# Cross-attention on one core: score weights by eleven block products in 64x64 tiles, and a loop of long and short steps

## The chip, the core and the metric

The kernel runs on one core of a Trainium2 chip, all in float32. The metric is device time in microseconds, lower is better. The engines are TensorE (PE in the profile, its weight loads PEld), VectorE (DVE), ScalarE (ACT), GpSimd (POOL) and SyncE (SP), which starts most of the transfers.

## The reference

There are B = 16 batches of 256 queries `x` (width 256) and 77 context rows `c` (width 192), and H = 8 heads of width 256. The mask is all ones. Cut to what matters:

```python
Q = (x @ Wq).reshape(B, -1, H, 256).transpose(0, 2, 1, 3)
K = (c @ Wk).reshape(B, -1, H, 256).transpose(0, 2, 1, 3)
V = (c @ Wv).reshape(B, -1, H, 256).transpose(0, 2, 1, 3)
score = jnp.einsum('bhqd,bhkd->bhqk', Q, K) / sqrt(256)
attn = softmax(where(mask, score, -inf), axis=-1)
out = einsum('bhqk,bhkd->bqhd', attn, V).reshape(B, -1, H * 256) @ Wo + x
return (out - mean(out)) * rsqrt(var(out) + 1e-5) * gamma + beta
```

## The kernel before

*Weights are combined first.* Per head, G = Wq Wk^T / 16 and U = Wv Wo are made once. G lies in `gA` (its first 128 context columns) and `gB` (the other 64, two heads to a tile), c turned in `cA` and `cB` in the same way. Then only A = G c ("a" tiles), scores = x A, and out = attn (c U) remain. A is made by groups of GB = 4 batches (NG = 4 groups): a *place* is two heads of one group, 16 places in all. `prepare_a` makes a place with 128x32 tiles over `cA` (L193) and 64x32 tiles over `cB` (L205), 308 columns each, into PSUM tiles `pa`, and ACT copies them out (L963). c U of one batch (`vw`) is `prepare_vw` (L227, L238).

*A step* is one batch b + 1: two tiles t of 128 queries. `scores` (L303, two PSUM banks per tile), `shift` (DVE, L320: adds the mask and keeps each head's greatest score, and releases the bank), `exponential` (ACT, L340), reciprocal (L355) and `weigh` (POOL, L361), `turn` (DVE transpose, L371). Then, for the batch before, `seven` (PE, L450): attn times `vw` for both tiles by seven block products instead of eight, into two banks `pm` and `po`; it needs `sums` of the turned weights (POOL, L431 to L434, tile `ss`) and `differences` of `vw` (POOL, L414, tile `ts`). ACT copies `pm` out as `m` (L475); `add_seven` adds `po` to x on DVE (`add_product`, L498) and `m` on POOL (L484). After that come mean and variance (`finish`, L506 and L509), `spread` (ACT, L527 and L528), and `normalise` (DVE, L548 and L577).

*Order.* PE, DVE, ACT, POOL and SP each run their instructions strictly as the program writes them (a manual schedule). The loop runs over b from -1 to 14; every second step ("ahead") prepares `vw` of two batches and two places of A. PE's order in a pair of steps is scores, `pv`, `pa`, `pv`, `pa`, `pv`, `pa`, `pv`, `pa`, `seven`, scores, `seven`. The 8 PSUM banks have one tag, `mm`, and go round: a product that takes a bank waits for whoever read the bank's last content. `turn_last` (L293) turns the last rows of `vw`, `transpose_x` (L165) the x tiles of a group ahead; `load_x` and `load_xT` start their transfers on SP.

## Time and profile before

| | |
|---|---|
| median of 3 runs | 271.01 us (270.75 to 271.03) |
| profiled execution, its span | 269.95 us, 268.2 us |
| busy, PE | 262.5 us |
| busy, PEld (weight loads) | 191.8 us |
| busy, DVE | 185.9 us |
| busy, POOL | 173.2 us |
| busy, ACT | 157.6 us |

The page gives the busy time of each engine; a row of a view of groups gives line, engine, operation, output and inputs, tile shape, count, then busy us and mean ns of one. A row of a timeline gives start, length, engine, line and count, and in brackets the idle time ahead with what ended it. Lengths of merged PE rows contain the end of a pipelined matmul, so the distance of two starts is the better measure. L numbers are lines of the kernel before.

### The profile page before, as it was taken

How to read it: one execution, taken by the hardware profiler on the slowest of the kernel's cores; microseconds unless marked ns; L12 is line 12 of the kernel's file. 1: busy time of each engine (PE TensorE's matmuls, PEld its weight loads, DVE VectorE, ACT ScalarE, POOL GpSimd, SP SyncE). 2: the span in 40 equal slices, each digit the busy share in tenths (PEclk: the TensorE clock that was granted, in tenths of full speed). 3: DMA queues.
4: the chain of work that ended last, by engine and by line, in shares of the span. 5: the costliest groups of instructions: out<-in, count | busy, mean ns of one | idle time of the engine just before them, and what ended most of it. 6: DMA issues, size and time to landing. Idle time of an engine off the chain costs nothing.

```text
span 268.2 us, 14455 instructions
## 1 busy us (share of the span) xinstructions
PE 262.5 (98%) x6090; PEld 191.8 (72%) x6090; DVE 185.9 (69%) x808; ACT 157.6 (59%) x667; POOL 173.2 (65%) x240
## 2 busy tenths in 40 slices
PE   8999999999999999999999999999999999999992
PEld 8566578944984699459944995499669957985662
DVE  1555967493583868665886379647977887799785
ACT  3243336536857565955596468737775595636772
POOL 1042005728399739994799669965998799585452
PEclk9999999999999999999999999999999999999999
DMA  6989987901500130232012401340034010100112
GB/s 190 217 199 228 334 138 142 311 21 34 129 7 2 46 80 2 63 111 71 5 43 90 112 5 43 91 113 2 6 120 122 4 45 2 44 22 22 46 40 80
DMA packets 41696, 22.69 MB, mean 85 GB/s; under 512 B 24144, under 2 KB 40608, under 8 KB 41632
## 3 DMA queue, kind: packets, MB, share of 16 engines
q1 hardware_dynamic: 41248, 20.98, 30.1%
q0 software_dynamic: 384, 0.79, 1.3%
q8 instruction: 48, 0.79, 1.3%
q14 instruction: 16, 0.13, 0.2%
HBM read 17.57 MB, written 4.19 MB: 81 GB/s over the span
## 4 chain that ended last, share of the span: by engine, by line
PE 98%; DVE 1%; issue 0%; DVEq 0%
PE ps L303 25%; PE pa L193 13%; PE pv L227 11%; PE po L450 11%; PE pm L450 8%; PE pa L205 6%; PE pv L238 6%; PE po L383 4%; PE pu L773 3%; PE pr L263 2%; PE pgb L834 2%; PE pw L787 1%; PE idle L703 1%; PE pr L274 1%; PE phb L850 1%; PE po L399 1%
## 5 line engine op out<-in xcount | busy, mean ns | idle before, releaser
L340 ACT ACTIVATE s<-s,top 128x77 f32<-128x77 f32 x256 | 85.3, 346 | 44.2 <-DVE top L320 37.9
L303 PE MATMUL ps<-a,xT 128*32 128x154 f32 x2048 | 69.9, 294 | 0.0
L303 PEld LDWEIGHTS ps<-a,xT 128*32 128x32 f32 x2048 | 66.2, 110 | 1.2 <-issue 0.4
L361 POOL TENSOR_TENSOR p<-s,rden 128x512 f32<-128x512 f32 x64 | 47.5, 768 | 29.5 <-DVE rden L355 29.4
L320 DVE CUSTOM_DVE_ANT_0 s<-ps,bias 128x77 f32<-128x77 f32 x256 | 43.5, 232 | 14.3 <-PE ps L303 14.3
L340 ACT ACTIVATION_READ_ACCUMULATOR s<-s,top 128x1 f32 x224 | 42.0, 187 | 0.0
L193 PE MATMUL pa<-cA,gA 128*32 128x308 f32 (+1 forms) x576 | 36.6, 395 | 0.0
L193 PEld LDWEIGHTS pa<-cA,gA 128*32 128x32 f32 x576 | 18.3, 110 | 21.0 <-issue 7.0
L484 POOL TENSOR_TENSOR xg<-xg,m 128x256 f32<-128x256 f32 x39 | 28.7, 736 | 6.6 <-DVE xg L498 4.5
L577 DVE SCALAR_TENSOR_TENSOR xg<-xg,rstd,bet 128x256 f32<-128x256 f32 x27 | 22.9, 847 | 14.0 <-ACT rstd L528 12.6
L227 PE MATMUL pv<-uA,cA 128*32 128x512 f32 x256 | 30.6, 595 | 0.0
L371 DVE STREAM_TRANSPOSE pT<-p 128x640 f32<-128x640 f32 x32 | 25.5, 821 | 3.4 <-POOL p L361 3.3
L414 POOL TENSOR_TENSOR ts<-vw 128x768 f32<-128x768 f32 x13 | 24.0, 1848 | 5.9 <-ACT vw L963 5.9
L963 ACT COPY vw<-pv 128x512 f32<-128x512 f32 x32 | 17.8, 584 | 14.8 <-PE pv L227 8.3
L498 DVE TENSOR_TENSOR xg<-po,xg 128x256 f32<-128x256 f32 x31 | 11.5, 405 | 13.8 <-PE po L450 13.3
L320 DVE DVE_READ_ACCUMULATOR2_ANT top<- 128x1 f32 x256 | 20.8, 81 | 0.0
L205 PE MATMUL pa<-cB,gB 64*32 64x308 f32 (+2 forms) x512 | 20.4, 387 | 0.0
L963 ACT COPY a<-pa 128x308 f32<-128x308 f32 (+1 forms) x56 | 18.9, 395 | 1.9 <-PE pa L193 0.4
L205 PEld LDWEIGHTS pa<-cB,gB 64*32 64x32 f32 (+1 forms) x512 | 11.0, 110 | 11.4 <-issue 6.2
L548 DVE SCALAR_TENSOR_TENSOR xg<-xg,mv,gam 128x256 f32<-128x256 f32 x30 | 17.6, 588 | 0.1
L238 PE MATMUL pv<-uB,cB 64*32 64x512 f32 x256 | 17.3, 597 | 0.0
L227 PEld LDWEIGHTS pv<-uA,cA 128*32 128x32 f32 x256 | 7.5, 109 | 12.8 <-issue 9.9
(119 smaller groups left out, 404.1 us busy)
## 6 DMA issues: line engine op xcount, KB each, us to landing
xg<-in_x_dram SPq DMA_DIRECT2D x8, 512.0 KB, 4.4
xT<-in_x_dram SPq DMA_DIRECT2D x56, 64.0 KB, 2.6
out_dram<-xg SPq DMA_DIRECT2D x11, 256.0 KB, 2.2
wo<-in_L_xattn_Wo_dram SPq DMA_DIRECT2D x4, 512.0 KB, 7.8
wq_blk<-in_L_xattn_Wq_dram SPq DMA_DIRECT2D x12, 128.0 KB, 4.3
out_dram<-xg SPq DMA_DIRECT2D x10, 128.0 KB, 1.9
wk_blk<-in_L_xattn_Wk_dram SPq DMA_DIRECT2D x12, 96.0 KB, 3.6
wvT<-in_L_xattn_Wv_dram POOLq DMA_DIRECT2D x8, 96.0 KB, 6.6
```

The source lines that it names most:

```text
L193: nc.tensor.matmul(flat(o[i * BK : (i + 1) * BK]), gA[:, h, cols(dc, i)], flat(cA[:, batches, :]), start=not rest_first and n in opening, ...
L205: nc.tensor.matmul(flat(banks[j + k][i * BK : (i + wide) * BK]), gB[half(k), h // 2, dc * P + i * BK : dc * P + (i + wide) * BK], flat(cB[ ...
L227: nc.tensor.matmul(pv[k][i * BK : (i + 1) * BK], cA[:, b, k * BK : (k + 1) * BK], uA[:, parts, :, i], start=not rest_first, stop=rest_first,)
L238: nc.tensor.matmul(pv[k][i * BK : (i + 1) * BK], cB[half(k), b, k * BK : (k + 1) * BK], uB[half(k), parts, :, i], start=rest_first, stop=n ...
L303: nc.tensor.matmul(ps[m // 2][i * BK : (i + 1) * BK, m % 2 * 2 * S2 : (m % 2 + 1) * 2 * S2], xT_of[t // PT][:, j * NM + m, dc], flat(a_of[ ...
L320: nc.vector.tensor_tensor_reduce(s[:, h], ps[a][:, k * S2 : (k + 1) * S2], bias[:, b, :], scale=-1.0, scalar=FAR, op0=ALU.add, op1=ALU.min ...
L340: nc.scalar.activation(s[:, h], s[:, h], AF.Exp, bias=top[:, one], scale=-1.0, accum_out=den[:, one] if summed_by_act(t) else None,)
L361: nc.gpsimd.tensor_tensor(part, e_mh[:, :, :, keys], rden_mh.unsqueeze(3).to_broadcast(list(part.shape)), ALU.mult,)
L371: nc.vector.transpose(pT_of[t].rearrange("p n m q -> p m n q"), p.rearrange("p m (n k) -> p m n k", k=BK),)
L450: nc.tensor.matmul(out[i * BK : (i + 1) * BK], weight[:, i], moving, start=first and n == 0, stop=final and n == len(terms) - 1,)
L484: nc.gpsimd.tensor_tensor(to, to, what, ALU.add)
L963: nc.scalar.copy(dst, src)
```

## The change

`prepare_fast` makes A for groups 1 to 3 (ten places with the whole of two heads; what is left of the last group goes the old way). Per head, G and c are seen as blocks of 64, A as 2x2 blocks (over dc, and over two halves of the four batches) plus the remaining 64 context columns; with sums of blocks of G (`gS`, `gC`) and of c (`cT`, `cD`) made ahead on ACT and POOL, 11 block products take the place of 12. Each is 64x64 and 154 columns wide; two heads are interleaved so that tiles at opposite corners of the array alternate. Per head there are two PSUM banks, `mids` and `ends` (tiles `pf`). The first product of each `mids` bank is copied out by ACT and its place used again; `put_together` makes the blocks of A by four additions on DVE.

The loop of the first 10 steps is written anew as `long_step` and `short_step`. In the long step PE's order is scores, `pv` over cA for two batches, `seven`, `pv` over cB, two fast places; the short step has scores and `seven`. In `scores_and_masks`, the mask pass of the first tile goes ahead of the preceding short step's last turn, sums and `add_seven` (`between`). Mean and variance of tiles of batches below 7 are made on ScalarE from accumulated sums. `normalise` is moved into later places, and the sums of c for the next group into two long steps.

**POOL, where a long step begins (b + 1 = 4; `ss_3` and `m_2`, `xg_1` are of the step before, `p` the weights of tiles 8 and 9).** Before:

```order
L361 TENSOR_TENSOR p_1_86<-s_7_1620,rden_7_1659 128x4x26
L414 TENSOR_TENSOR ts_3_1667<-vw_3_1378 128x768
L484 TENSOR_TENSOR m_2_1735<-m_2_1735 128x128 x2
L484 TENSOR_TENSOR xg_1_518<-xg_1_518,m_2_1735 128x256
L484 TENSOR_TENSOR xg_1_518<-xg_1_518,m_2_1735 128x2x128
L484 TENSOR_TENSOR xg_1_518<-xg_1_518,m_2_1735 128x256
L431 TENSOR_TENSOR ss_3_1750<-pT_7_1741 128x256
L432 TENSOR_TENSOR ss_3_1750<-pT_7_1741,pT_6_1739 128x256
L433 TENSOR_TENSOR ss_3_1750<-pT_7_1741,ss_3_1750 128x256
L434 TENSOR_TENSOR ss_3_1750<-pT_6_1739,ss_3_1750 128x256
L361 TENSOR_TENSOR p_0_85<-s_8_1823,rden_8_1917 128x4x128
L361 TENSOR_TENSOR p_0_85<-s_8_1823,rden_8_1917 128x4x26
```

With the change:

```order
L602 TENSOR_TENSOR ss_3_1916<-pT_7_1914 128x256
L603 TENSOR_TENSOR ss_3_1916<-pT_7_1914,pT_6_1831 128x256
L604 TENSOR_TENSOR ss_3_1916<-pT_7_1914,ss_3_1916 128x256
L605 TENSOR_TENSOR ss_3_1916<-pT_6_1831,ss_3_1916 128x256
L655 TENSOR_TENSOR m_2_1814<-m_2_1814 128x128 x2
L655 TENSOR_TENSOR xg_1_532<-xg_1_532,m_2_1814 128x256
L655 TENSOR_TENSOR xg_1_532<-xg_1_532,m_2_1814 128x2x128
L655 TENSOR_TENSOR xg_1_532<-xg_1_532,m_2_1814 128x256
L532 TENSOR_TENSOR p_0_88<-s_8_1904,rden_8_2188 128x4x128
L532 TENSOR_TENSOR p_0_88<-s_8_1904,rden_8_2188 128x4x26
L532 TENSOR_TENSOR p_1_89<-s_9_1928,rden_9_2192 128x4x128
L532 TENSOR_TENSOR p_1_89<-s_9_1928,rden_9_2192 128x4x26
```

The weighing of tile 7 (`p_1`, `s_7`) and `ts_3` now come ahead of this stretch; the sums `ss_3` go ahead of `m_2` and `xg_1`, and the weighing of both tiles of the long step stands behind all of them.

**DVE, behind the reciprocals of the same step (`po_3` is the bank that `seven` filled, `xT_3` an x tile of a group ahead).** Before:

```order
L355 RECIPROCAL rden_9_1933<-den_9_1921 128x8
L548 SCALAR_TENSOR_TENSOR xg_1_518<-xg_1_518,mv_0_1346,gam_69 128x256
L577 SCALAR_TENSOR_TENSOR xg_1_518<-xg_1_518,rstd_4_1944,bet_90 128x256
L371 STREAM_TRANSPOSE pT_8_2086<-p_0_85 128x4x5x32
L371 STREAM_TRANSPOSE pT_9_2088<-p_1_86 128x4x5x32
L165 STREAM_TRANSPOSE xT_3_1441<-xT_3_1441 128x512 x2
L548 SCALAR_TENSOR_TENSOR xg_1_518<-xg_1_518,mv_0_1346,gam_69 128x256
L577 SCALAR_TENSOR_TENSOR xg_1_518<-xg_1_518,rstd_4_1944,bet_90 128x256
L498 TENSOR_TENSOR xg_1_518<-po_3_2017,xg_1_518 128x256 x2
```

With the change:

```order
L526 RECIPROCAL rden_8_2188<-den_8_1938 128x8
L526 RECIPROCAL rden_9_2192<-den_9_1947 128x8
L542 STREAM_TRANSPOSE pT_8_2196<-p_0_88 128x4x5x32
L542 STREAM_TRANSPOSE pT_9_2198<-p_1_89 128x4x5x32
L669 TENSOR_TENSOR xg_1_532<-po_3_1990,xg_1_532 128x256 x2
L725 SCALAR_TENSOR_TENSOR xg_0_530<-xg_0_530,mv_0_1569,gam_69 128x256
L754 SCALAR_TENSOR_TENSOR xg_0_530<-xg_0_530,rstd_2_1964,bet_93 128x256
L174 STREAM_TRANSPOSE xT_3_1620<-xT_3_1620 128x512 x2
L372 TENSOR_TENSOR a_2_2073<-pf_2_0_0_2074,a_2_2073 128x2x77
L372 TENSOR_TENSOR a_2_2073<-pf_2_0_0_2074,a_2_2073 128x4x77
L372 TENSOR_TENSOR a_2_2073<-pf_2_0_0_2074,a_2_2073 128x2x77
L372 TENSOR_TENSOR a_2_2073<-pf_2_0_0_2075,a_2_2073 128x6x77
```

The statistics are gone, the two additions of `po_3` (L669) stand directly behind the turns of tiles 8 and 9, and behind the moved normalise and x turns come the new additions of `put_together` (L372), the first four of twelve.

**PE, the end of `seven` and the first fast place (`pf_2_0_0`, `pf_2_1_1`: banks of heads 0 and 1 of group 2; waits in brackets name the engine that PE waits for).** Before, the rows with waits of `pv` and `pa` ahead of `seven`, and the first row behind them:

```order
L303 MATMUL ps_9_1_1790<-a_1_838,xT_2_960 32x154 [waits DVE_49,PE_49]
L227 MATMUL pv_4_0_1850<-uA_79,cA_81 32x512 [waits DVE_49,PE_49]
L227 MATMUL pv_4_1_1851<-uA_79,cA_81 32x512 [waits DVE_49,PE_49]
L193 MATMUL pa_2_0_0_0_1853<-cA_81,gA_77 32x308 [waits Activation_49]
L193 MATMUL pa_2_1_0_0_1854<-cA_81,gA_77 32x308 [waits DVE_49,PE_49]
L193 MATMUL pa_2_0_1_0_1855<-cA_81,gA_77 32x308 [waits DVE_49,PE_49]
L193 MATMUL pa_2_1_1_0_1856<-cA_81,gA_77 32x308 [waits DVE_49,PE_49]
L238 MATMUL pv_4_0_1850<-uB_80,cB_82 32x512
```

With the change, the end of `seven`, the last row of `pv`, and of the fast place the rows with waits and some that follow them:

```order
L621 MATMUL po_3_1990<-vw_3_1362,ss_3_1916 32x128 [waits Pool_49]
L621 MATMUL po_3_1990<-vr_804,pT_7_1914 32x256 x4
L621 MATMUL po_3_1990<-ts_3_1606,pT_7_1914 32x128 x8
L403 MATMUL pv_5_0_1971<-uB_83,cB_85 32x512
L360 MATMUL pf_2_0_0_2075<-cA_84,gA_77 64x154 [waits DVE_49,PE_49]
L360 MATMUL pf_2_0_0_2074<-cA_84,gA_77 64x154 [waits DVE_49,PE_49]
L360 MATMUL pf_2_1_1_2077<-cA_84,gA_77 64x154 [waits Activation_49]
L360 MATMUL pf_2_1_1_2076<-cA_84,gA_77 64x154 [waits DVE_49,PE_49]
L360 MATMUL pf_2_1_1_2077<-cA_84,gS_519 64x154
L360 MATMUL pf_2_0_0_2075<-cT_79,gA_77 64x154
L360 MATMUL pf_2_1_1_2077<-cT_79,gA_77 64x154
```

Where the products of A waited for ACT and for banks that DVE's mask passes release, the third pair of the fast place's products (`pf_2_1_1_2076`) now takes the bank of `po_3` and waits for the second addition of L669.

```diff
--- before.py
+++ after.py
+    KX = HB * S2
+    FAST = NG - 1
+    low, high = slice(0, LB), slice(LB, P)
+    cT = const.tile([P, 4, FAST, KX], F32, tag="cT", name="cT")
+    cD = const.tile([P, FAST, KX], F32, tag="cD", name="cD")
+    gC = const.tile([P, NF, P], F32, tag="gC", name="gC")
...
-            return slice((2 * i + dc) * BK, (2 * i + dc + 1) * BK)
+            return slice(dc * P + i * BK, dc * P + (i + 1) * BK)
...
+    def sums_of_g():
+        for parts, sums, e, own, other in parts_of_g():
+            nc.scalar.copy(sums[own, 0, e], parts[other, 1, e])
+            nc.scalar.copy(gC[own], gB[other, :, P:])
+        for parts, sums, e, own, other in parts_of_g():
+            s1, s2, s3 = (sums[own, n, e] for n in range(3))
+            add(s1, s1, parts[own, 1, e])
+            subtract(s2, s1, parts[own, 0, e])
+            subtract(s3, parts[own, 0, e], parts[own, 1, e])
...
+    def sums_of_c(lo, hi):
+        xs, ys = halves_of(cA, lo, hi)
+        t1, t2, t3, t4 = (cT[:, n, lo - 1 : hi - 1] for n in range(4))
+        subtract(t1, ys, xs)
+        for own, other in ((low, high), (high, low)):
+            nc.gpsimd.tensor_copy(t2[own], ys[other])
+        subtract(t3, t2, ys)
+        subtract(t2, t2, t1)
+        for own, other in ((low, high), (high, low)):
+            nc.gpsimd.tensor_copy(t4[own], t2[other])
+        subtract(t4, xs, t4)
...
+        for e, h in enumerate(heads):
+            for banks in (mids, ends):
+                banks.append(ps_mm.tile([P, 3, KX], F32, tag="mm", name=f"pf_{g}_{h}_{len(ends)}"))
...
+        def middle(e):
+            h, own = heads[e], (high, low)[e]
+            return [
+                ((mids[e], 2), from_g(own, h, 0), c_of(cA, own, xs)),
+                ((mids[e], 0), from_s(own, 0, h), t_of(own, 0)),
+                ((mids[e], 2), from_s(own, 1, h), t_of(own, 1)),
+                ((mids[e], 1), from_s(own, 2, h), t_of(own, 2)),
+                (
+                    (mids[e], 1),
+                    lambda i: gC[own, u, half(i)],
+                    c_of(cB, own, ys),
+                ),
+            ]
+        def outer(e):
+            h, own = heads[e], (low, high)[e]
+            return [
+                ((ends[e], 0), from_g(own, h, 0), c_of(cA, own, xs)),
+                ((ends[e], 1), from_s(own, 0, h), c_of(cA, own, ys)),
+                ((ends[e], 2), from_g(own, h, 1), t_of(own, 3)),
+                ((ends[e], 0), from_rest(h, 0), c_of(cB, own, xs)),
+                ((ends[e], 1), from_rest(h, 0), c_of(cB, own, ys)),
+                ((ends[e], 2), from_rest(h, 1), cD[own, g - 1]),
+            ]
+        def pairs():
+            o, m = outer(0), middle(1)
+            ones = o[:2] + m[:1] + o[2:] + m[1:]
+            o, m = outer(1), middle(0)
+            return list(zip(ones, m[:1] + o[:3] + m[1:] + o[3:]))
+        def products():
+            total = {id(bank): 6 for bank in ends} | {id(bank): 5 for bank in mids}
+            lone = {id(bank): e for e, bank in enumerate(mids)}
+            seen = dict.fromkeys(total, 0)
+            for pair in pairs():
+                flags = []
+                for (bank, _), _, _ in pair:
+                    key = id(bank)
+                    n, seen[key] = seen[key], seen[key] + 1
+                    one = key in lone and n == 0
+                    flags.append(
+                        (one or n == (key in lone), one or n == total[key] - 1, one)
+                    )
+                for i in range(2):
+                    for ((bank, n), weight, moving), (start, stop, _) in zip(pair, flags):
+                        nc.tensor.matmul(
+                            bank[half(i), n],
+                            weight(i),
+                            moving,
+                            start=start,
+                            stop=stop,
+                        )
+                for ((bank, n), _, _), (_, _, one) in zip(pair, flags):
+                    if one:
+                        nc.scalar.copy(blocks[lone[id(bank)]][:, 0], by_batch(bank)[:, n])
+        def plus(out, *of):
+            nc.vector.tensor_tensor(out, *of, ALU.add)
+        def put_together(e):
+            mid, end, of = by_batch(mids[e]), by_batch(ends[e]), blocks[e]
+            plus(of[:, 3], mid[:, 2], of[:, 0])
+            plus(of[:, 1:3], mid[:, 0:2], of[:, 3:4].to_broadcast([P, 2, HB, S2]))
+            plus(of[:, 3], mid[:, 0], of[:, 2])
+            plus(of[:, 0:3], end, of[:, 0:3])
+        return products, put_together
...
+    def by_act(t):
+        return t // QT < B - 2 * GB - 1
+    def fast(b):
+        return b < B - GB - GB // 2
...
+        if by_act(t):
+            junk = st.tile([P, DI], F32, tag="junk", name=f"junk_{t}", bufs=1)
+            mean, var = (mv_of[g][:, j, n : n + 1] for n in range(2))
+            nc.scalar.activation(junk, y, AF.Identity, scale=1.0 / DI, accum_out=mean)
+            nc.scalar.activation(junk, y, AF.Square, bias=mean, scale=-1.0, accum_out=var)
+            return
...
-        if g < NG - 1 or g == NG - 1 and n < NF // 2:
-            work.append(prepare_a(g, (n,), rest_first=rest_first))
-        elif b <= NS:
+        if b <= NS and not fast(b):
...
+    def statistics(tiles):
+        for t in tiles:
+            finish(t)
+        if tiles:
+            spread(tiles[0], tiles[-1] + 1)
+            invert(tiles[0], tiles[-1] + 1)
+    between = []
+    def scores_and_masks(new, to_finish=()):
+        for t in new:
+            scores(t)
+        for i, t in enumerate(new):
+            shift(t)
+            for t in to_finish[i : i + 1]:
+                finish(t)
+            while between:
+                between.pop(0)()
+    def long_step(b):
+        now, new = tiles_of(b), tiles_of(b + 1)
+        g, n = (b + 1) // GB + 1, (b + 1) % GB
+        if now:
+            scores_and_masks(new)
+            for t in new:
+                exponential(t)
+        for m in range(0, 2) if b < 0 else range(b + 2, min(b + 3, B // 2)):
+            turn_last(m)
+        statistics(tiles_of(b - 2))
+        works = work_of(b + 1) + work_of(b + 2)
+        for part_A, *_ in works:
+            part_A()
+        if now:
+            seven(b)
+        for _, part_B, _ in works:
+            part_B()
+        fasts = []
+        for k in range(2):
+            fasts.append(prepare_fast(g, n + k))
+            if k == 0:
+                copy_out(works[:1])
+            fasts[k][0]()
+            if k == 0:
+                copy_out(works[1:])
+        statistics(tiles_of(b - 1))
+        if now:
+            for t in new:
+                weigh(t)
+        for t in new:
+            turn(t)
+        if b < 0:
+            for t in range(QT, GT, 2):
+                transpose_x(t)
+            sums(b + 1)
+            differences(b + 1)
+            bias_of(GB, B)
+            differences(b + 2)
+        else:
+            sums(b + 1)
+            add_seven(b)
+            for k in range(2):
+                differences(b + 1 + k)
+            if n == 2 and g < NG - 1:
+                sums_of_c(g + 1, g + 2)
+        for t in tiles_of(b - 2):
+            normalise(t)
+        turn_some_x(g, n)
+        if g < NG:
+            load_x((g * GB + n) // 2)
+            for k in range(2):
+                load_xT(g * GT + (n + k) * QT, g * GT + (n + k + 1) * QT, after_pool=k == 0)
+        fasts[0][1](0)
+        fasts[0][1](1)
+        fasts[1][1](0)
+        behind.append(partial(fasts[1][1], 1))
+        for t in tiles_of(b - 1):
+            behind.append(partial(normalise, t))
+    def short_step(b):
+        new = tiles_of(b + 1)
+        scores_and_masks(new)
+        for t in new:
+            exponential(t)
+        seven(b)
+        weigh(new[0])
+        for _ in range(2):
+            if behind:
+                behind.pop(0)()
+        for m in range(b + 2, min(b + 3, B // 2)):
+            turn_last(m)
+        weigh(new[1])
+        turn(new[0])
+        while behind:
+            behind.pop(0)()
+        def last_turn():
+            turn(new[1])
+            sums(b + 1)
+            add_seven(b)
+        between.append(last_turn)
+    ready = B - GB - GB // 2 - 1
+    for b in range(-1, ready, 2):
+        long_step(b)
+        short_step(b + 1)
...
```

More of the change, by code (lines that the diff above doesn't have):

```diff
@@ L216, in prepare_a, with parts_of_g @@
         return part_A, part_B, copies
+    add, subtract = (
+        partial(nc.gpsimd.tensor_tensor, op=op) for op in (ALU.add, ALU.subtract)
+    )
+    def parts_of_g():
+        parts = gA.rearrange("p (u e) (dc i c) -> p dc e u i c", e=2, dc=2, c=BK)
+        sums = gS.rearrange("p n (u e) (i c) -> p n e u i c", e=2, c=BK)
+        return [(parts, sums, e, own, other) for e, own, other in ((0, high, low), (1, low, high))]
+    def sums_of_g():
[7 more added lines that the diff above has]
+            subtract(s3, parts[own, 0, e], parts[own, 1, e])
@@ new lines, in last_sums_of_g, with halves_of @@
+    def last_sums_of_g():
+        for parts, sums, e, own, other in parts_of_g():
+            nc.scalar.copy(sums[other, 0, e], sums[own, 1, e])
+        for parts, sums, e, own, other in parts_of_g():
+            subtract(sums[other, 0, e], parts[other, 0, e], sums[other, 0, e])
+    def halves_of(c, lo, hi):
+        groups = c[:, lo * GB : hi * GB].rearrange("p (g y b) k -> p y g (b k)", y=2, b=HB)
+        return groups[:, 0], groups[:, 1]
+    def sums_of_c(lo, hi):
[9 more added lines that the diff above has]
+        subtract(t4, xs, t4)
@@ L526, in spread @@
         rstd = st.tile([P, GT], F32, tag="rstd", name=f"rstd_{first}")
-        nc.scalar.activation(log[:, lo:hi], mv_of[g][:, lo:hi, 1], AF.Ln, bias=eps)
+        nc.scalar.activation(log[:, lo:hi], mv_of[g][:, lo:hi, 1], AF.Ln, bias=eps, scale=1.0 / DI if by_act(first) else 1.0)
         nc.scalar.activation(rstd[:, lo:hi], log[:, lo:hi], AF.Exp, scale=-0.5)
@@ L893 @@
             a_of_pairs(a, rest_first=True)
+        gS = const.tile([P, 3, H, P], F32, tag="gS", name="gS")
+        sums_of_g()
         load_x(0)
@@ L971, in turn_x_and_normalise @@
                 transpose_x(to_turn[0] * GT + j)
+    def turn_x_and_normalise(g, n, old):
+        turn_some_x(g, n)
         if old:
@@ L976, with tiles_of @@
     last = NT - 1
-    for b in range(-1, B - 1):
+    def tiles_of(b):
+        return range(b * QT, (b + 1) * QT) if b >= 0 else ()
+    def statistics(tiles):
[14 more added lines that the diff above has]
+                between.pop(0)()
@@ L978 @@
+    ready = B - GB - GB // 2 - 1
+    for b in range(-1, ready, 2):
+        long_step(b)
+        short_step(b + 1)
+    statistics(tiles_of(ready - 2))
+    behind.extend(partial(normalise, t) for t in tiles_of(ready - 2))
+    for b in range(ready, B - 1):
         old = range(max(b - 1, 0) * QT, b * QT)
@@ L980 @@
         new = range((b + 1) * QT, (b + 2) * QT)
-        for t in new if b >= 0 else ():
-            scores(t)
-        for t in new if b >= 0 else ():
-            shift(t)
-            if b == B - 2:
-                finish(t - 2 * QT)
+        scores_and_masks(new, old if b == B - 2 else ())
         while behind:
@@ L991 @@
             load_x((g * GB + n) // 2)
-        for m in range(0, 2) if b < 0 else range(b + 2, min(b + 3, B // 2)):
-            turn_last(m)
         alone = b + 1 >= B - GB // 2
-        works = work_of(b + 1) if alone or n % 2 == 0 else []
-        for part_A, _, _ in works:
+        ahead = not alone and n % 2 == 0
+        works = work_of(b + 1) if alone or ahead else []
+        for part_A, *_ in works:
             part_A()
@@ L1017 @@
             break
-        for i, t in enumerate(new if b >= 0 else ()):
+        for i, t in enumerate(new):
             exponential(t)
-            if old:
-                finish(old[i])
+            finish(old[i])
             weigh(t)
-        ahead = works and not alone
-        if old and not ahead:
-            spread(old[0], old[-1] + 1)
         if ahead:
             copy_out(works)
-            if old:
-                spread(old[0], old[-1] + 1)
+        spread(old[0], old[-1] + 1)
+        if ahead:
             works = work_of(b + 2, rest_first=True)
@@ L1032 @@
                 part_B()
-            for part_A, _, _ in works:
+            for part_A, *_ in works:
                 part_A()
@@ L1040 @@
         if b < NS:
-            if now:
-                seven(b)
-            if old:
-                invert(old[0], old[-1] + 1)
-                normalise(old[0])
+            seven(b)
+            invert(old[0], old[-1] + 1)
+            normalise(old[0])
             for t in new:
                 turn(t)
-            if b < 0:
-                for t in range(QT, GT, 2):
-                    transpose_x(t)
-                bias_of(GB, B)
             if alone or ahead:
@@ L1059 @@
                 sums(b + 1)
-            if now:
-                add_seven(b)
+            add_seven(b)
             if b + 1 < NS and not ahead:
```

43 lines of the change are left out of this document (37 added, 6 removed).

## The prediction

> **What bounds the kernel now.** I read the page's busy shares and its chain first, then the busy time of the engines in one steady stretch, then the order of PE's work there.
>
> ```profile
> PE 262.5 (98%) x6090; PEld 191.8 (72%) x6090; DVE 185.9 (69%) x808; ACT 157.6 (59%) x667; POOL 173.2 (65%) x240
> PE 98%; DVE 1%; issue 0%; DVEq 0%
> 102.70:130.60 27.90, 27.90 (x716) 20.24 (x710) 19.23 (x97) 18.18 (x83) 22.26 (x30) 1.00 0.22 60
> ```
>
> The chain that ends last is PE almost from end to end. In the third row (a stretch of two steps: PE, PEld, DVE, ACT, POOL, granted clock, DMA share) PE has no idle time, while POOL works 22.26 of 27.90 us and DVE 19.23. So only PE work saved can make the kernel faster, and another engine can only cost time: POOL has 5.6 us of room per pair of steps, DVE 8.7. Whether that room suffices is a question of order, since both queues run strictly in the order written. PE's two steps, by start and length:
>
> ```profile
> 74.81 4.37 PE L303 MATMUL ps<-a,xT 128*32 128x154 f32 x128
> 79.00 1.90 PE L227 MATMUL pv<-uA,cA 128*32 128x512 f32 x16
> 80.72 2.26 PE L193 MATMUL pa<-cA,gA 128*32 128x308 f32 x32
> 82.91 1.09 PE L238 MATMUL pv<-uB,cB 64*32 64x512 f32 x16
> 83.79 1.24 PE L205 MATMUL pa<-cB,gB 64*32 64x308 f32 x32
> 84.83 1.06 PE L238 MATMUL pv<-uB,cB 64*32 64x512 f32 x16
> 85.68 1.24 PE L205 MATMUL pa<-cB,gB 64*32 64x308 f32 x32
> 86.86 1.92 PE L227 MATMUL pv<-uA,cA 128*32 128x512 f32 x16
> 88.60 2.26 PE L193 MATMUL pa<-cA,gA 128*32 128x308 f32 x32
> 90.67 0.62 PE L450 MATMUL pm<-vw,pT 128*32 128x128 f32 x16
> ...
> 94.59 4.37 PE L303 MATMUL ps<-a,xT 128*32 128x154 f32 x128
> ...
> 102.70 4.37 PE L303 MATMUL ps<-a,xT 128*32 128x154 f32 x128
> ```
>
> Starts give the true durations: scores 4.19, `pv` over cA 1.72, `pa` over cA 2.07 (88.60 to 90.67), `pv` over cB 0.86, `pa` over cB 1.04 (83.79 to 84.83), `seven` 3.92 (90.67 to 94.59), the pair 27.89 (74.81 to 102.70). A place of A (two heads of one group) thus costs 2.07 + 1.04 = 3.11 us.
>
> **The change: PE's share.** A fast place issues 88 records of 154 columns in 64x64 tiles. If four of them run side by side, that is 22 groups. The 128 records of scores, 32 groups of 154 columns, took 4.19, or 0.131 a group. That 64x64 tiles do run by fours is seen in the setup:
>
> ```profile
> 13.29 1.10 PE L850 MATMUL phb<-qT,kT_all 64*64 64x128 f32 x32
> 14.22 1.91 PE L834 MATMUL pgb<-qT,kT_all 64*64 64x256 f32 x32
> 15.94 1.22 PE L205 MATMUL pa<-cB,gB 64*64 64x308 f32 x16
> ```
>
> Eight groups took 0.93 at 128 columns (0.116 each) and 1.72 at 256 (0.215); at 154 columns the line between gives 0.136. So a place takes 22 x 0.131 = 2.88 to 22 x 0.136 = 2.99, against 3.11; I take 2.88, the row of the same width: 0.23 saved per place, 0.46 per pair. A switch of tile shape shows where a row runs over its own rate: 2.19 instead of 2.07 at 80.72 and 1.18 instead of 1.04 at 85.68, about 0.15 each, two per pair. The long step has three (128x32 to 64x32, to 64x64, back), so 0.15 of it goes again. **PE alone: 27.89 - 0.46 + 0.15 = 27.6 a pair; ten fast places are five pairs, 1.5 us gained in all** (0.7 with 0.136).
>
> [...]
>
> **The change: the queues.** The eight ACT copies of A per pair are replaced by four `put_together` on DVE, each four dependent adds of 154, 308, 154 and 462 columns from PSUM and SBUF; The four lone copies and eight passes of statistics that ACT gets instead are at most 1 us each (an exponential of 77 columns takes 0.36, below; a pass has 256), so with the eight copies gone they fit into ACT's 9.7 us of room; if they did not, the copy of `m` would be late, and PE with it. Nearest rows for the adds, and for the other DVE work:
>
> ```profile
> L498 DVE TENSOR_TENSOR xg<-po,xg x31: 378/408/425, 76.5 to 261.2; 128x256 f32<-128x256 f32 x31
> L516 DVE TENSOR_TENSOR xg<-po,xg 128x128 f32<-128x128 f32 x2 | 0.6, 286 | 0.0
> L577 DVE SCALAR_TENSOR_TENSOR xg<-xg,rstd,bet x27: 483/840/1760, 86.9 to 264.9; 128x256 f32<-128x256 f32 x27
> L371 DVE STREAM_TRANSPOSE pT<-p 128x640 f32<-128x640 f32 x32 | 25.5, 821 | 3.4 <-POOL p L361 3.3
> L165 DVE STREAM_TRANSPOSE xT<-xT 128x512 f32<-128x512 f32 x16 | 10.1, 668 | 0.0
> ```
>
> The line through 128 columns at 286 and 256 at 408 gives 0.31, 0.45, 0.31 and 0.60, with 0.035 between them **1.7 us a put** (bounds 1.45, if they overlap like the two adds of 408 that took 0.72 at 105.04 below, and 1.9). POOL works beside some of them. L577 spreads from 483 to 1760 ns and L498 only from 378 to 425, and a put reads as L498 does, PSUM and one operand in SBUF; slowed as L577's median is against its least (840/483), it would take 3.0, which I keep for a rival. [...]
>
> Below, a normalise is 0.43 (at 101.98) and L577's median of 0.84, so 1.3 beside a busy POOL (bounds 1.2, and 1.4 if its first half is slowed a little too), and 1.0 where POOL waits (101.98 to the end at 103.00).
>
> ```profile
> 95.89 0.24 DVE L320 CUSTOM_DVE_ANT_0 s<-ps,bias 128x77 f32<-128x77 f32 x1 [0.29 <-PE ps L303]
> 96.93 0.24 DVE L320 CUSTOM_DVE_ANT_0 s<-ps,bias 128x77 f32<-128x77 f32 x1 [0.32 <-PE ps L303]
> 101.98 0.43 DVE L548 SCALAR_TENSOR_TENSOR xg<-xg,mv,gam 128x256 f32<-128x256 f32 x1
> 102.52 0.48 DVE L577 SCALAR_TENSOR_TENSOR xg<-xg,rstd,bet 128x256 f32<-128x256 f32 x1
> 105.04 0.72 DVE L498 TENSOR_TENSOR xg<-po,xg 128x256 f32<-128x256 f32 x2
> 105.68 0.22 DVE L320 CUSTOM_DVE_ANT_0 s<-ps,bias 128x77 f32<-128x77 f32 x1
> 108.21 0.08 DVE L320 DVE_READ_ACCUMULATOR2_ANT top<- 128x1 f32 x1
> ```
> ```profile
> 105.99 0.99 POOL L484 TENSOR_TENSOR m<-m 128x128 f32<-128x128 f32 x2
> 106.93 2.41 POOL L484 TENSOR_TENSOR xg<-xg,m 128x256 f32<-128x256 f32 x3
> 112.76 2.89 POOL L361 TENSOR_TENSOR p<-s,rden 128x512 f32<-128x512 f32 x4
> 117.44 0.73 POOL L431 TENSOR_TENSOR ss<-pT 128x256 f32<-128x256 f32 x1
> 120.01 0.73 POOL L434 TENSOR_TENSOR ss<-pT,ss 128x256 f32<-128x256 f32 x1
> ```
> ```profile
> 96.23 0.36 ACT L340 ACTIVATE s<-s,top 128x77 f32<-128x77 f32 x1 [2.92 <-DVE top L320]
> 98.99 0.35 ACT L340 ACTIVATE s<-s,top 128x77 f32<-128x77 f32 x1
> ```
>
> Two mask passes take 2.53 (105.68 to 108.21), one 1.27; eight exponentials 2.76, the first 0.34 after its mask. Before, POOL weighs `p_8` and `p_9` as soon as their reciprocals are there, and only later come the sums of that step. In the change the preceding step's sums, `m` and `xg` stand ahead of them: 3.30 (117.44 to 120.74) + 0.99 + 2.41, then 2.89 for the weighing, **9.6 us of POOL**. On DVE the turns of `p_8` and `p_9` wait for it, and behind them stand the two adds that release the bank `po_3`. The third pair of the fast place's products (two tiles side by side, eight records, two groups) goes into that bank: a wait that PE did not have.
>
> *Even without any lag it bites.* From the start of the long step's scores PE reaches that pair at 4.19 + 3.44 + 3.92 + 0.15 + 1.72 + 0.15 + 0.52 (two pairs, four groups) = 14.1 us. The queues: the mask of the second bank starts 2.34 in (96.93 after 94.59) and takes 0.63; turn 0.82, to 3.8; POOL 9.6, to 13.4; turn of `p_9` 0.8, adds 0.72: 15.0. **PE stalls 0.9.**
>
> *And the lag grows*, because the two queues form a ring, POOL to DVE and back. From one pair to the next, by the order in which they stand: POOL 9.6; turn 0.82; adds 0.72; two normalise beside POOL 2.6; two turns of x 1.3; three puts 5.1; two mask passes and the wait for the first tile's exponentials 0.34 + 2.76 + 0.2 = 3.3; the fourth put 1.7; a normalise 1.0; `vr`, as wide as x's turn, 0.7; reciprocals 0.1; turn 0.82; the other normalise 1.0; the first mask pass of the next long step 1.27; turn 0.82. The sum is 30.8, less some 0.3 for the overlap of neighbours: **30.5, against PE's 27.6**. While the ring is shorter than PE, PE leads; here it is longer by 2.9, and PE follows. Mask passes hide nothing for it: their banks too wait for the puts ahead of them.
>
> The five pairs: the first, whose long step has no scores, 27.6; the second 27.6 + 0.9 = 28.5; the third starts with DVE 1.1 us late, 29.6; the fourth and fifth at the ring's 30.5. Sum 146.7 against 5 x 27.89 = 139.45: **7.2 us more**. The fifth pair's backlog (some 4 us of DVE and POOL) is taken up by the steps after, which keep the old order and POOL's 5.6 us of room; if not, it is lost once, 4. The sums of G and c fall before the steady stretch, where POOL is freer (65% over the whole span, 80% in the stretch); what stuck out of its idle time would be added one to one. The loads of x and of its transposed tiles move together into the long step on SP's queue:
>
> ```profile
> xT<-in_x_dram SPq DMA_DIRECT2D x56, 64.0 KB, 2.6
> ```
>
> At 2.6 us each and a DMA share of 0.22 they are hidden behind the steps that lie between them and their scores; uncovered, one would cost 2.6. I take nothing for all three. The profiled execution was 269.95 and the median of the runs 271.01, 1.06 above. So 269.95 + 7.2 + 1.06 = **278**. With every row at its short bound (POOL 9.0, put 1.45, normalise 1.2) the pairs come to 140.9, +1.4, 272.4; with the long ones (1.9, 1.4) to 149.3, +9.8, 281.
>
> **Rivals.** *The queues keep up*: only PE's share counts, 269.95 - 1.5 + 1.06 = 269.5. For it: the busy sums fit, POOL's 22.3, and DVE's 19.2 + 4 x 1.7 = 26.0 before the statistics are taken off, both under 27.6. Against it: the ring counts what stands in a row, not busy time; it needs to be 3 us shorter than the rows say. *A small lag cancels the gain*: 0.3 a pair, ring 27.9 to 28: about 271. *POOL slows the puts*: one mechanism, at the four puts of a pair, if they lengthen beside a reading POOL as L577 does. At 3.0 each the ring is 5.2 longer, and the last three pairs cost some 15 more, 290; half of that 285. Against it is L498's narrow spread. *Tiles do not run by fours*: one group's products taking turns two by two would add 2.9 a place, 29 us; the eight-group rows exclude it almost.
>
> **Numbers.** The long ring 0.70 (272.4 to 281 its own range, 278 predicted); queues keep up 0.16; small lag 0.06; slowed puts or tiles 0.08. Under 0.2% (0.54 us) a measurement of this kernel cannot tell from none. Faster, 269.5, is then 0.17, the same 0.07, slower 0.76. The range 269.4 to 283 leaves out the slow rival and about half of the fast one.
>
> **What would show it.** PE idle ahead of the fast products, released by DVE's add of `po`: 0.9 in the second long step, 2.5 to 3 in the fourth; pairs of 28.5, 29.6, 30.5. DVE there idle only behind POOL's weighing. A put of 1.7, and 2.9 for a fast place that isn't waiting. I am wrong if PE shows no idle time in the long steps, or if it waits for a lone copy of ACT or a setup sum instead.

## The result and the profile after

The changed kernel takes 279.78 us (median of 4 runs, 279.64 to 279.92) against 270.88 us before (4 runs, 270.62 to 271.03): **slower, ratio 1.033, 95% interval 1.0312 to 1.0348**. Forecast were 278.0, range 269.4 to 283.

The page of the changed kernel, busy times and chain:

```profile
PE 264.4 (95%) x6330; PEld 206.4 (74%) x6330; DVE 208.6 (75%) x860; ACT 166.1 (60%) x710; POOL 191.6 (69%) x272
PE 35%; DVE 28%; POOL 20%; ACT 7%; DMA 4%; issue 4%; SPq 1%; DVEq 0%; POOLq 0%; ACTq 0%
```

PE's share of the span fell from 98% to 95%, but its share of the chain that ends last fell from 98% to 35%: DVE and POOL have taken its place, although neither is busy for more than 75%. The four pairs of steps with scores, cut at the starts of their long steps' scores (columns: PE, PEld, DVE, ACT, POOL, granted clock, DMA share, GB/s):

```profile
74.88:102.97 28.09, 27.82 (x760) 22.62 (x756) 20.28 (x98) 18.98 (x89) 23.31 (x36) 1.00 0.09 27
102.97:132.92 29.95, 28.02 (x758) 22.89 (x754) 23.28 (x102) 18.72 (x86) 21.98 (x30) 1.00 0.26 68
132.92:165.19 32.27, 29.89 (x766) 25.97 (x758) 25.54 (x108) 21.95 (x104) 25.07 (x39) 0.95 0.15 44
165.19:194.47 29.28, 28.02 (x757) 22.66 (x753) 21.66 (x100) 19.20 (x88) 21.04 (x28) 1.00 0.24 65
```

They took 119.6 us where four pairs took 111.5 before (4 x 27.88), 8.1 of the 9.3 us by which the span grew (277.5 against 268.2). PE's waits, from the view that sums them by what ended them (us in all, times, longest):

```profile
PE pf L360 <- DVE xg L669: 5.1, 4, 2.1
...
PE pm L621 <- POOL ss L604: 0.3, 1, 0.3
```

The first row is the forecast wait: the fast products `pf`, for DVE's additions of `po`, once in each of the four long steps. Why those additions are late is read from DVE and from POOL, from one pair to the next:

```profile
107.50 0.84 DVE L542 STREAM_TRANSPOSE pT<-p 128x640 f32<-128x640 f32 x1
...
116.12 0.84 DVE L542 STREAM_TRANSPOSE pT<-p 128x640 f32<-128x640 f32 x1 [3.70 <-POOL p L532]
117.46 0.85 DVE L542 STREAM_TRANSPOSE pT<-p 128x640 f32<-128x640 f32 x1 [0.49 <-POOL p L532]
118.23 0.72 DVE L669 TENSOR_TENSOR xg<-po,xg 128x256 f32<-128x256 f32 x2
118.87 0.59 DVE L725 SCALAR_TENSOR_TENSOR xg<-xg,mv,gam 128x256 f32<-128x256 f32 x1
...
121.98 1.29 DVE L174 STREAM_TRANSPOSE xT<-xT 128x512 f32<-128x512 f32 x2
123.20 5.42 DVE L372 TENSOR_TENSOR a<-pf,a 128x154 f32<-128x154 f32 x12
...
131.88 1.80 DVE L372 TENSOR_TENSOR a<-pf,a 128x154 f32<-128x154 f32 x4
...
138.41 0.84 DVE L542 STREAM_TRANSPOSE pT<-p 128x640 f32<-128x640 f32 x1
```
```profile
108.42 0.73 POOL L602 TENSOR_TENSOR ss<-pT 128x256 f32<-128x256 f32 x1 [2.39 <-DVE pT L542]
...
112.39 2.36 POOL L655 TENSOR_TENSOR xg<-xg,m 128x256 f32<-128x256 f32 x3
114.71 2.72 POOL L532 TENSOR_TENSOR p<-s,rden 128x512 f32<-128x512 f32 x4
118.45 0.73 POOL L602 TENSOR_TENSOR ss<-pT 128x256 f32<-128x256 f32 x1 [1.02 <-DVE pT L542]
...
139.32 0.74 POOL L602 TENSOR_TENSOR ss<-pT 128x256 f32<-128x256 f32 x1 [2.39 <-DVE pT L542]
```

The ring stands there. The last turn of a short step (107.50) releases POOL, which then works for 9.0 us (108.42 to 117.43), and DVE waits 3.70 us for the first part of its weighing. From there DVE goes, with no wait of more than 0.6 us, through the turns, the additions, two normalise, the turns of x, the `put_together` additions (L372) and the mask passes between them, up to the next last turn (138.41), for which POOL waits 2.39 us. From last turn to last turn, one round of the ring, it is 30.91 us, against PE's 27.6.

### The profile page after: what moved, and what is told of

The parts are those of the page before. It is cut to its first block, busy times and chain, and to the rows that moved or that the text cites. A ratio compares the mean times of both kernels' runs of the same rounds, so it can differ in the third digit from the quotient of the medians.

```text
span 277.5 us, 15091 instructions
## 1 busy us (share of the span) xinstructions
PE 264.4 (95%) x6330; PEld 206.4 (74%) x6330; DVE 208.6 (75%) x860; ACT 166.1 (60%) x710; POOL 191.6 (69%) x272
## 4 chain that ended last, share of the span: by engine, by line
PE 35%; DVE 28%; POOL 20%; ACT 7%; DMA 4%; issue 4%; SPq 1%; DVEq 0%; POOLq 0%; ACTq 0%
PE pf L360 7%; ACT s L511 7%; PE ps L468 6%; POOL p L532 6%; DVE pT L542 5%; DVE a L372 5%; POOL xg L655 4%; DVE s L485 4%; DVE xg L754 4%; DVE xg L725 3%; PE pa L202 3%; PE pu L950 3%; PE pv L392 3%; PE pr L428 2%; POOL ts L585 2%
## 5 line engine op out<-in xcount | busy, mean ns | idle before, releaser
L485 DVE CUSTOM_DVE_ANT_0 s<-ps,bias 128x77 f32<-128x77 f32 x256 | 42.3, 230 | 0.9 <-PE ps L468 0.8
L372 DVE TENSOR_TENSOR a<-pf,a 128x154 f32<-128x154 f32 x80 | 33.8, 432 | 3.6 <-PE pf L360 0.9
L392 PE MATMUL pv<-uA,cA 128*32 128x512 f32 x256 | 29.7, 593 | 0.0
L754 DVE SCALAR_TENSOR_TENSOR xg<-xg,rstd,bet 128x256 f32<-128x256 f32 x27 | 18.8, 695 | 3.1 <-ACT rstd L705 1.2
L602 POOL TENSOR_TENSOR ss<-pT 128x256 f32<-128x256 f32 x13 | 9.7, 746 | 16.5 <-DVE pT L542 16.4
L725 DVE SCALAR_TENSOR_TENSOR xg<-xg,mv,gam 128x256 f32<-128x256 f32 x30 | 19.5, 651 | 0.1
L360 PE MATMUL pf<-cT,gS 64*64 64x154 f32 x240 | 18.8, 306 | 0.0
L392 PEld LDWEIGHTS pv<-uA,cA 128*32 128x32 f32 x256 | 9.3, 110 | 12.2 <-issue 8.9
L360 PEld LDWEIGHTS pf<-cT,gS 64*64 64x64 f32 x240 | 17.0, 140 | 0.0
L621 PE MATMUL po<-vr,pT 128*32 128x256 f32 x208 | 16.6, 379 | 0.0
L360 PE MATMUL pf<-cA,gA 64*64 64x154 f32 x160 | 11.0, 301 | 5.1 <-DVE xg L669 5.1
```

The costliest lines, as they stand in the source:

```text
L360: nc.tensor.matmul(bank[half(i), n], weight(i), moving, start=start, stop=stop,)
L372: nc.vector.tensor_tensor(out, *of, ALU.add)
L392: nc.tensor.matmul(pv[k][i * BK : (i + 1) * BK], cA[:, b, k * BK : (k + 1) * BK], uA[:, parts, :, i], start=not rest_first, stop=rest_first,)
L485: nc.vector.tensor_tensor_reduce(s[:, h], ps[a][:, k * S2 : (k + 1) * S2], bias[:, b, :], scale=-1.0, scalar=FAR, op0=ALU.add, op1=ALU.min ...
L725: nc.vector.scalar_tensor_tensor(y, y, mv_of[t // GT][:, t % GT, 0:1], gam, ALU.subtract, ALU.mult)
L754: nc.vector.scalar_tensor_tensor(y, y, rstd, bet, ALU.mult, ALU.add)
```

## The experiments

The theory: this ring of two queues, each waiting for the other, sets the period; the bank of `po` is only where PE feels it. The main rivals: that one wait is the whole loss; DVE simply has too much work; the statistics on ScalarE; the new loop by itself. Each run has the kernel before beside it on the same chip (medians 270.3 to 270.7 us), so that the changed kernel's own 279.8 stands some 0.3 us lower on their scale, at 279.5.

### The additions of the po bank ahead of the turns (a1)

```diff
         if now:
             for t in new:
                 weigh(t)
+            for t in tiles_of(b):
+                add_product(t)
         for t in new:
             turn(t)
```

(`add_seven` leaves out the additions that are already made)

> Edit: in the long step the two additions of the po bank stand ahead of the turns of the new tiles on DVE instead of behind them; nothing else moves. Theory (a POOL-DVE ring of 30.9 us per pair, as the trace of the changed kernel shows between two turns, 107.50 and 138.41): the wait of the fast products for that bank goes (0.3, 1.8, 2.1 and 0.8 us in the change), but the ring only loses these 0.7 us, 30.2 against PE's 27.6, so PE waits elsewhere, for the sums or for banks held by the put_together additions: a gain of 2 to 4 us, 276 to 278. Rival (that one bank's wait is the whole loss): 27.6 a pair, 270 to 271.

Measured: 276.88 us, some 3 us better than the change and far from 270. PE's waits in this run:

```profile
PE ps L468 <- issue: 3.8, 3, 1.4
...
PE pm L621 <- POOL ss L604: 0.8, 1, 0.8
PE ps L468 <- DVE a L372: 0.5, 1, 0.5
```

The wait for the `po` bank is gone, and others stand in its place: 3.8 us at the scores of three short steps and 0.5 at those of a long one, and 0.8 for the sums. The row with "issue" names no releaser; DVE's row at one of the three shows what it may be:

```profile
151.65 5.41 DVE L372 TENSOR_TENSOR a<-pf,a 128x154 f32<-128x154 f32 x12
```

In this step PE stood from 151.47 to 152.90 ahead of the scores, until 1.25 us into these additions, about as long as the first three take (0.31, 0.48, 0.31), and these read the first `pf` bank. That the scores wait for this bank is read from the times and not shown by the view. The last turns still follow each other by 29.2 to 30.1 us. That one wait was not the loss.

### The idle time of DVE filled (a2)

```diff
+        for t in tiles_of(b - 2):
+            normalise(t)
+        turn_some_x(g, n)
+        if now:
+            for t in tiles_of(b):
+                add_product(t)
         for t in new:
             turn(t)
...
-        for t in tiles_of(b - 2):
-            normalise(t)
-        turn_some_x(g, n)
```

(and `statistics(tiles_of(b - 2))` moved from the long step to the end of the short step ahead of it)

> Edit: in the long step the normalise of two tiles, the two turns of x and the two additions of the po bank all stand ahead of the turns of the new tiles, in the 3.7 us in which DVE waits for POOL's weighing; the statistics these normalise need are made a short step earlier. Theory (ring): the ring loses 2.4 + 1.3 + 0.7 = 4.4 us, 26.5 a pair, under PE's 27.6; PE no longer waits and the fast products' saving shows: 269 to 270.5, at or a little under the kernel before. Rival (too much work on DVE: the put_together additions cost what they take, wherever they stand): no more than 2 us better than the change, 277.5 to 280.

Measured: 271.62 us, ratio to the kernel before 1.0042 (1.0026 to 1.0058): 8 us better than the change with the same instructions, 1 us above the expected range. So it isn't the amount of DVE's work. What was left: PE still waited 0.8 us in all for the additions, and 1.1 us for the sums of one step, where POOL and DVE show this:

```profile
156.92 0.46 POOL L265 TENSOR_TENSOR cT<-cA 128x154 f32<-128x154 f32 x1
...
160.21 0.46 POOL L272 TENSOR_TENSOR cT<-cA,cT 128x154 f32<-128x154 f32 x1
```
```profile
162.27 0.85 DVE L542 STREAM_TRANSPOSE pT<-p 128x640 f32<-128x640 f32 x1 [3.07 <-POOL p L532]
```

The sums of c for a later group, 3.8 us on POOL, stand ahead of a weighing that DVE needs.

### The same extra work inside and outside the ring (a3, a4)

```diff
+        if now:
+            for _ in range(4):
+                nc.vector.transpose(bet, bet)
```

In a3 it stands behind the turns of x, ahead of `put_together`; in a4 ahead of the turns of the new tiles, where DVE waits for POOL.

> Edit: four idle turns of a 128x256 constant (even in number, so it is unchanged) on DVE in each of the four long steps with scores, about 1.3 us, placed in the ring, ahead of the put_together additions. Theory: the ring binds in the last three pairs, so +1.3 for two to four of them, +2.6 to +5: 282.5 to 285. Rival (only the wait for the po bank counts, and it lies ahead of this place): within 0.5 of the change, 279.3 to 280.3.

> Edit: the same four idle turns per long step, but ahead of the turns of the new tiles, where DVE waits 3.7 us for POOL. Theory: nothing, 279.3 to 280.3. Rival (DVE's busy time is what costs): as in the ring, +2.6 to +5.

Measured: 284.45 us in the ring, 279.04 us in the gap. The four idle turns as they stand in a3, and the wait ahead of the first turn of a new tile in a4:

```profile
123.49 1.84 DVE L1234 STREAM_TRANSPOSE bet<-bet 128x256 f32<-128x256 f32 x4
```
```profile
116.17 0.84 DVE L542 STREAM_TRANSPOSE pT<-p 128x640 f32<-128x640 f32 x1 [1.93 <-POOL p L532]
```

They take 1.8 us, not the 1.3 of the expectation. In the gap they only shorten DVE's wait, from 3.70 to 1.93 us, and the last turns follow each other by 30.89 and 30.29 us, as in the change (30.91 and 30.30). In the ring the same two rounds take 32.65 and 32.04 us, each 1.74 more. So the same four instructions in each long step cost nearly 5 us at one place and nothing at the other. DVE's busy time is not what counts; its place is.

### A version without waits (b1)

```diff
         for t in tiles_of(b - 2):
             normalise(t)
-        turn_some_x(g, n)
         if now:
             for t in tiles_of(b):
                 add_product(t)
+        turn_some_x(g, n)
...
         weigh(new[1])
+        if b < ready - 1:
+            sums_of_c(2 + b // 4, 3 + b // 4, b // 2 % 2)
         turn(new[0])
```

(on a2; the last argument chooses the first or the second half of the sums, and the long step's call is gone)

> Edit on a2: the additions of the po bank stand ahead of the two turns of x (the fast products still waited 0.2 to 0.4 us for them), and the sums of c for a later group, 3.6 us of POOL that in a2 stood ahead of a short step's weighing and made DVE wait 3.1 us, are cut in halves and put behind the weighing of four short steps, where POOL waits 2.4 us for DVE anyway. Theory (ring): no wait is left on PE in the four pairs, 27.6 us each against 28.0, 28.0 and 29.5 in a2: 268.5 to 269.7, 0.3 to 0.8 per cent under the kernel before. Rival (what is left in a2 lies elsewhere, in the setup or the last steps): 271 to 272.

Measured: 269.20 us, **ratio to the kernel before 0.9954 (0.994 to 0.9967): this version beats both kernels**, the kernel before by half a per cent (its slowest run took 269.78, the fastest of the kernel before beside it 270.15). Its pairs:

```profile
75.40:102.99 27.59, 27.59 (x761) 22.66 (x757) 20.17 (x99) 18.97 (x89) 22.39 (x33) 1.00 0.11 31
102.99:130.57 27.58, 27.58 (x760) 22.65 (x755) 24.97 (x104) 20.60 (x95) 23.43 (x33) 1.00 0.21 60
...
158.16:185.75 27.59, 27.59 (x761) 22.65 (x756) 23.28 (x103) 20.58 (x95) 23.23 (x33) 1.00 0.22 61
```

PE has no idle time in them. DVE is busier than in the kernel before by up to 5.7 us a pair (24.97 against 19.23), and this costs nothing.

### The old products in the new loop (b2)

```diff
-            fasts.append(prepare_fast(g, n + k))
+            fasts.append(prepare_a(g, (n + k,)))
...
             fasts[k][0]()
+            fasts[k][1]()
...
+            copy_out(fasts[k:])
...
-        fasts[0][1](0)
-        fasts[0][1](1)
-        fasts[1][1](0)
-        behind.append(partial(fasts[1][1], 1))
```

> Edit: the loop of the change, but A by the old twelve products with eight copies on ACT; put_together is gone from DVE. Theory (ring): it loses the 6.8 us of four put_together, 24 a pair, under PE's 28.0; only up to 0.4 us a pair is left of the wait for the po bank: 271 to 273. Rival (the new loop's order costs by itself, whatever makes A): 277 to 280.

Measured: 274.63 us, between theory and rival. PE's order there:

```profile
89.02 2.28 PE L202 MATMUL pa<-cA,gA 128*32 128x308 f32 x32
91.23 1.27 PE L214 MATMUL pa<-cB,gB 64*32 64x308 f32 x32
92.42 2.28 PE L202 MATMUL pa<-cA,gA 128*32 128x308 f32 x32
94.64 1.27 PE L214 MATMUL pa<-cB,gB 64*32 64x308 f32 x32
95.83 0.46 PE L468 MATMUL ps<-a,xT 128*32 128x154 f32 x6
```

The two places take 6.81 us (89.02 to 95.83), not 2 x 3.11: each of the four rows is followed by another tile shape, and each is 0.14 or 0.15 us over its rate (2.07 and 1.04 in the prediction). The expectation had left these switches out; with them PE alone needs 28.48 a pair (between the starts of the first two long steps' scores, with no wait), by estimate 3.0 us more than before over five pairs. The next three pairs took 28.89, 28.75 and 28.80, another 1.0 us; together that is the 4 us above the kernel before. Without `put_together` in the ring the large waits are gone.

### Statistics on DVE again (b3)

```diff
     def by_act(t):
-        return t // QT < B - 2 * GB - 1
+        return False
```

> Edit: mean and variance of all tiles on DVE again, in the places where the change has them on ScalarE. Theory (ring): the statistics of the batch before wait on DVE for POOL's additions to x and stand ahead of the reciprocals, so POOL's weighing starts some 1.5 us later in each ring: three ring-bound pairs, 282.5 to 285. Rival (the passes on ScalarE hold up its exponentials and copies, and that is the loss): 272 to 278.

Measured: 282.50 us, at the lower edge of the theory's range. The move of the statistics to ScalarE helped the change by some 3 us (the rounds are 0.85 to 0.88 us longer here than in the change); it is no part of the loss.

### The last turn ahead of the mask pass again (b4, c2, d1)

```diff
-        between.append(last_turn)
+        last_turn()
```

> Edit: the last turn of a short step, its sums and add_seven stand at the end of that step again, ahead of the next step's first mask pass. Theory (ring): one mask pass of 1.3 us leaves the ring, 29.6 a pair, but the mask pass is late by some 3 us, and a bank that pv needs with it: 276.5 to 279.5. Rival (that this order is what made the change slow): 270 to 273. Rival (it is what keeps it from being slower): 282 or more.

Measured on the changed kernel: 274.53 us, 5 us better than the change and 2 us better than the theory's range. The turns follow each other by 28.4 to 29.7 us, as the theory had it; the price it gave for the late mask pass (a bank that `pv` needs) isn't there. So in the change's own order, taking the mask pass from ahead of the last turn wins back 5 of the 9 us. (This does not add up with the gains of the other runs, which shorten the same ring.) Does that hold in another order too? On b1:

> Edit on b1: the last turn of a short step stands ahead of the next step's first mask pass again, as in b4. Theory (ring): the ring is already no longer than PE's 27.6, so shortening it by a mask pass gives nothing: within 0.5 of b1, 268.7 to 269.8. Rival (b4 gained 5 us for another reason, which would show here too): 2 us or more under b1.

Measured: 271.67 us, 2.5 us *worse* than b1; neither theory nor rival had this. DVE in the same long step of b1 and then of c2, the second reciprocal and the additions of `po` (scores start at 130.57 and at 130.91):

```profile
139.20 0.20 DVE L528 RECIPROCAL rden<-den 128x8 f32<-128x8 f32 x1 [1.24 <-ACT s L513]
...
142.37 0.76 DVE L672 TENSOR_TENSOR xg<-po,xg 128x256 f32<-128x256 f32 x2
```
```profile
141.34 0.20 DVE L528 RECIPROCAL rden<-den 128x8 f32<-128x8 f32 x1 [2.54 <-ACT s L513]
...
145.08 0.74 DVE L672 TENSOR_TENSOR xg<-po,xg 128x256 f32<-128x256 f32 x2
```

With the last turn first, the reciprocal comes 10.4 us into the step instead of 8.6, since mask passes and exponentials start later. Behind it come the normalise and the additions: they begin 14.2 us in instead of 11.8 and end at 14.9, while PE, by the sum in the prediction, reaches the bank at 14.1. The long steps that start at 102.67, 130.91 and 159.84 take 0.3, 1.0 and 0.3 us more than b1's 19.46, and each short step behind them 0.3 more than b1's 8.13. To see whether this is the cause, d1 puts the additions ahead of the normalise:

```diff
             for t in new:
                 weigh(t)
-        for t in tiles_of(b - 2):
-            normalise(t)
-        if now:
             for t in tiles_of(b):
                 add_product(t)
+        for t in tiles_of(b - 2):
+            normalise(t)
         turn_some_x(g, n)
```

> Edit on c2: the additions of the po bank stand ahead of the two normalise instead of behind them. In c2's trace a DVE chain ends at these additions: the last turn and its additions first, so the mask passes end 1.9 us later, so the exponentials and the second reciprocal, then 3.6 us of normalise, and the additions at 145.08, just as PE needs the bank. Theory (that chain is why c2 is 2.5 us above b1): with the additions ahead of the normalise the fast products no longer wait (0.3, 1.0 and 0.3 us in c2), and of the 0.3 us a pair at seven at least a part stays, since the turns come later: 269.5 to 271. Rival (c2 waits for POOL's weighing, as the change does): no better than c2, 271.3 to 273.

Measured: 273.01 us, worse again; this is the rival's number, but not its mechanism, since DVE does not wait for POOL's weighing ahead of the turns of the new tiles. The fast products no longer wait for the bank, as expected, and the long steps take 19.46 us again, as in b1. The short steps behind them take 9.0 to 9.8 us instead of 8.1:

```profile
PE pm L623 <- POOL ts L587: 2.9, 3, 1.5
```

DVE now stands idle for PE's `po` (7.4 us in all, in c2 2.0) instead of working on the normalise, so the turns of the new tiles come 0.2 to 0.4 us later in the step, with them POOL's sums and behind those its `differences` (tile `ts`), for which the short step's `seven` waits; and PE, no longer held up, is there earlier. The chain to the additions was real, but not the whole price: without the mask pass ahead, this order has no room left, and the wait removed shows as the next one. Which of the two orders is better depends on what else stands in the gap.

### Idle times of PE and the granted clock (c1)

```diff
         if now:
+            for _ in range(b + 5):
+                nc.vector.transpose(bet, bet)
             for t in tiles_of(b):
                 add_product(t)
```

> Edit on b1: 6, 8, 10 and 12 idle turns of a 128x256 constant stand on DVE ahead of the additions of the po bank in the four long steps, so that PE stands idle there for about 1.4, 2.2, 2.9 and 3.7 us. Question: does an idle time of over 2.1 us by itself halve the granted clock for some 3.4 us, as behind the 2.13 us in the changed kernel and not behind its 1.83? Theory (it does): clock 0.5 behind the second, third and fourth gap, 1.7 us more for each: some 284. Rival (the dip there was chance): clock 1.00 throughout, some 279.

Measured: 283.21 us in one run. The first gap did not arise (that pair took 27.59 us, as in b1); the others, each with the stretch behind it (the granted clock is the third number from the end):

```profile
116.35:119.19 2.84, 0.00 (x1) 0.03 (x1) 2.70 (x8) 0.10 (x1) 0.00 (x0) 1.00 0.14 33
119.19:123.90 4.71, 4.71 (x93) 4.71 (x97) 4.11 (x8) 1.40 (x4) 1.98 (x3) 0.64 0.28 95
148.68:151.46 2.78, 0.00 (x0) 0.03 (x1) 2.64 (x8) 0.09 (x1) 0.00 (x0) 1.00 0.03 8
151.46:156.00 4.54, 4.54 (x140) 4.54 (x144) 4.40 (x10) 2.65 (x8) 1.80 (x3) 1.00 0.37 118
179.62:184.43 4.81, 0.00 (x1) 0.03 (x1) 4.54 (x12) 0.09 (x1) 0.00 (x0) 1.00 0.42 108
184.43:188.20 3.77, 3.77 (x64) 3.77 (x68) 2.87 (x6) 1.26 (x3) 1.11 (x2) 0.55 0.01 5
```

The clock fell behind the gaps of 2.84 and 4.81 us (0.64 and 0.55 over the stretches shown, 0.50 within them), not behind the one of 2.78 (1.00). Neither theory nor rival holds as put: two of these three idle times had a dip behind them, one had none.

## Why the prediction was right

**PE's share: right.** A pair without waits takes 27.59 (b1), forecast 27.6. The same row in the first and in the second fast place of a long step of b1:

```profile
89.77 0.44 PE L362 MATMUL pf<-cT,gA 64*64 64x154 f32 x8
...
92.65 0.44 PE L362 MATMUL pf<-cT,gA 64*64 64x154 f32 x8
```

They are 2.88 us apart, as forecast. The changed kernel shows the gain where no queue is in the way: from the scores of batch 0 to those of batch 1 it takes 24.53 us (42.22 to 66.75), before 24.86 (41.85 to 66.71).

**The cost of a put: right, a little small.** The additions by their shape in the changed kernel:

```profile
L372 DVE TENSOR_TENSOR a<-pf,a 128x462 f32<-128x462 f32 x20 | 12.8, 640 | 1.4 <-DVE a L372 0.5
L372 DVE TENSOR_TENSOR a<-pf,a 128x154 f32<-128x154 f32 x40 | 12.2, 306 | 1.6 <-PE pf L360 0.9
L372 DVE TENSOR_TENSOR a<-pf,a 128x308 f32<-128x308 f32 x20 | 9.6, 479 | 0.7
```

Forecast were 0.31, 0.45, 0.31 and 0.60; a put takes 1.80 (row 131.88), not 1.7. The rival in which POOL slows them (3.0 a put) is out: all 80 additions lie between 262 and 642 ns, the longest form takes 640 in the mean, and a put takes 1.80 too where POOL is busy from its start to its end (162.77 to 164.57).

**The ring: right, 30.9 against 30.5**, with two terms off in opposite ways. A normalise beside POOL took 1.55 (118.87 to 121.98 for two, POOL busy for 2.95 of the 3.11) where 1.3 was put in, while one with POOL idle took 0.99 (133.59 to 134.58), forecast 1.0; POOL's chain took 9.0 where 9.6 was. The four puts add 0.4.

**The wait for the `po` bank: right in place, too large.** Without lag, forecast 0.9 in the second pair's long step, measured 0.27: POOL's 9.6, again, was 0.6 too much. With the lag, 2.5 to 3 were forecast for the fourth pair's long step, measured 2.13; the third has 1.83 and the fifth 0.82.

**The growth: right in sum.** Pairs of 28.5, 29.6, 30.5 and 30.5 were forecast, 119.1 in all; measured 28.09, 29.95, 32.27 and 29.28, 119.6. The ring itself is nearer to the forecast than the single pairs: its rounds take 29.64, 30.91 and 30.30 us, from the last turn at 77.86 over 107.50 and 138.41 to this one:

```profile
168.71 0.84 DVE L542 STREAM_TRANSPOSE pT<-p 128x640 f32<-128x640 f32 x1
```

That the third pair is long and the fourth short is a thing the prediction did not have: the clock, 0.95 over the third pair and 1.00 over the other three, below. "The backlog costs nothing" was wrong by 1.2 us (from 194.47 to the end 83.0, before from 186.34 on 81.9).

**ACT at nothing: right.** No wait of PE in that view of the changed kernel names ACT, and b3 shows the statistics better off there.

**The rival "the queues keep up" lost for the reason given**: room by busy time is no room in a row. Its price, 269.5, was right for the kernel that it describes: b1, with the same work in another order, took 269.2. What the prediction did not single out is how much of the ring was the mask pass ahead of the last turn (b4: 5 us). It stood in the sum with 1.27 a pair, and b4's three rounds are 1.21 to 1.26 us shorter than the change's, 3.7 in all; where the rest of the 5 comes from stays open (b4 also has no dip of the clock: 1.00 in every stretch of 2 us up to 186).
